# Larger field loads on the software queue, lent as output tiles until they are needed

## The chip, the core and the metric

The kernel runs on one core of a Trainium2 chip. A core has TensorE (PE) for matrix products, VectorE (DVE), ScalarE (ACT) and GpSimd (POOL) for elementwise work, and SyncE (SP), which here only issues DMA transfers. Transfers between the off-chip memory and the on-chip memory (128 partitions) are carried by sixteen DMA engines. A transfer can be issued from SyncE or ScalarE (the hardware queues q1 and q10 of the profile) or from GpSimd (the software queue q0). The metric is the device time of one execution in microseconds; lower is better. The kernel before takes 747.88 us (median of three runs, 745.85 to 748.31).

## The reference

There are 1024 samples with 32 fields of 128 numbers each, and for each of the 496 pairs of fields i < j a matrix W of 128x128:

```python
v_i = inputs[:, I_IDX, :]
v_j = inputs[:, J_IDX, :]
transformed = jnp.einsum('bpd,ped->bpe', v_i, W)
return transformed * v_j
```

For every pair the field i is multiplied by the pair's matrix and the result, element by element, by the field j. All is in float32. The inputs are 49 MB, the output is 260 MB.

## The kernel before, in words

**Tiles.** Everything is transposed: the 128 numbers of a field lie on the partitions and the 1024 samples along the row. A field is a tile of 128x1024 floats (512 KB), a weight load brings the matrices of eight pairs (`WL = 8`, 512 KB), and an output tile holds the results of four pairs (`OG = 4`, 2 MB). The pairs are taken with i from 30 down to 0 and j from i+1 to 31, numbered q = 0 to 495. So the fields with high numbers are needed first, and a field f is first needed when i reaches it: for fields 16, 12, 8 and 4 at the pairs 105, 171, 253 and 351. Each pair is done in two halves of 512 samples; half number u belongs to pair u // 2.

**A half.** For the first 15 pairs one matrix product in float32 is used (L203). After that, products are made of three parts: field and weights are each split into a high, a low and a difference part. `split_w` (L127 to L136) does this for two pairs' weights: ScalarE makes the high part (L132), GpSimd the others (L133 to L135). `split_x` (L141) does it for a field in two halves: ScalarE at L147, GpSimd at L148, L149 and, for later fields, L153; for the earlier ones VectorE makes the difference (L261). `first(u)` runs two of the products (L206) and ScalarE scales the sum in the accumulator (L207). `second(u - LAG)`, three halves later, adds the third product (L215), and VectorE multiplies by the field j into the output tile (L221). Two halves after a tile's last multiplication ScalarE issues its store (L254).

**Order.** The order is written by hand: the loop at L230 goes over the halves and appends to each engine's instructions (`tc.manual_schedule()`). Each engine works through its own in order and waits by semaphores where data or a buffer isn't ready. The splits are taken from a list, one per pair, by the pair at which they are allowed and the pair at which they are due. The splits of a field i may come at the earliest one pair after the row of i+1 has begun.

**Buffers.** Output tiles come from a pool of three (`opool`, L81), raw weight chunks from a pool of three (`rpool`), split weights from a pool of four. Each field has a tile of its own for the whole run.

**Loads.** Fields 30 to 15 and field 0 come one by one through SyncE or ScalarE (`load_x`, L86). Fields 1 to 14 come two at a time by `load_x_apart` (L109), and seven weight chunks (`WAPART`, L39) in the same way, by `load_apart` (L105): the first 112 rows are issued from GpSimd (L106), arranged so that the outermost dimension is `NE = 14`, and the other 16 rows from SyncE (L107). The host reorders those rows beforehand, so that the kernel reads them back in place. Three pairs later `move_on` (L101) issues a scrap of a load, with two rows, from GpSimd (L103). It has no use as data: [...] The first such call has five rows and the last has 13. All other weight chunks come whole from SyncE (L123), up to 12 pairs ahead of use.

Of the kernel before, what the change touches and what calls it, by code (L numbers as in the profile page):

```python
# [7 lines left out]
F32 = mybir.dt.float32  # L8
# [3 lines left out]
P = 128  # L12
NF = 32
NQ = NF * (NF - 1) // 2
BT = 1024
HB = 512
WC = 2
WL = 8
OG = 4
# [7 lines left out]
XAFTER = 54  # L27
XLEAD = 5

NE = 14
ROWS = 8 * NE
XAPART = 14
XSTEP, XPOS = 4, 8
WAPART = (45, 47, 49, 51, 54, 58, 60)  # L39
BACK = 3  # L40
SLAG = 2


# [6 lines left out]
def kernel(  # L50
# [26 lines left out]
    xpool = ctx.enter_context(tc.tile_pool(name="x", bufs=1))  # L77
    spool = ctx.enter_context(tc.tile_pool(name="xs", bufs=2))
    rpool = ctx.enter_context(tc.tile_pool(name="wr", bufs=WB))
    wpool = ctx.enter_context(tc.tile_pool(name="ws", bufs=4))  # L80
    opool = ctx.enter_context(tc.tile_pool(name="o", bufs=3))  # L81
    ppool = ctx.enter_context(tc.tile_pool(name="ps", bufs=8, space=bass.MemoryType.PSUM))

    x_sb = {}

    def load_x(f, pieces=1, eng=None):  # L86
        if f == 0:

            t = rpool.tile([P, WL, P], F32, tag="w", name="x_0").rearrange("p q e -> p (q e)")
        else:  # L90
            t = xpool.tile([P, BT], F32, tag=f"x{f}", name=f"x_{f}")
        s = BT // pieces
        for k in range(pieces):
            (eng or nc.sync).dma_start(out=t[:, k * s : (k + 1) * s], in_=xt[f, :, k * s : (k + 1) * s])
        x_sb[f] = t
# [5 lines left out]
    def move_on(k):  # L101

        nc.gpsimd.dma_start(out=mark[: 2 * k], in_=xt[0, : 2 * k, :16].rearrange("(b a) n -> a b n", a=k))  # L103

    def load_apart(dst, src):  # L105
        nc.gpsimd.dma_start(out=dst[:ROWS], in_=src[:ROWS].rearrange("(b a) m n -> a b m n", a=NE))  # L106
        nc.sync.dma_start(out=dst[ROWS:], in_=src[ROWS:])  # L107

    def load_x_apart(f):  # L109

        t = xpool.tile([P, 2, BT], F32, tag=f"x{f}", name=f"x_{f}")
        rows = xt[f : f + 2].rearrange("m d b -> (m d b)").rearrange("(d m b) -> d m b", m=2, b=BT)
        load_apart(t, rows)
        for k in range(2):
            x_sb[f + k] = t[:, k, :]

    def load_w(c, splits=(0, WL), eng=nc.sync):
        w_raw[c] = rpool.tile([P, WL, P], F32, tag="w", name=f"w_{c}")
        if c in WAPART:
            load_apart(w_raw[c], wt[c])  # L120
            return
        for a, b in zip(splits, splits[1:]):
            eng.dma_start(out=w_raw[c][:, a:b, :], in_=wt[c, :, a:b, :])  # L123
# [33 lines left out]
    first_q = {i: q for q, (i, j) in reversed(list(enumerate(pairs)))}  # L157
# [30 lines left out]
    w_q = {c: q for q, c in w_at.items()}  # L188
    back = []


    ctx.enter_context(tc.manual_schedule())
    po, ots, stores = {}, {}, []


    def first(u):
        q, h = divmod(u, 2)
        i, c = pairs[q][0], q // WC
        r = slice(q % WC * P, (q % WC + 1) * P)
        s = slice(h * HB, (h + 1) * HB)  # L200
        po[u] = ppool.tile([P, HB], F32, tag="po", name=f"po_{u}")
        if q < nq0:
            nc.tensor.matmul(po[u], w_raw[q // WL][:, q % WL, :], x_sb[i][:, s], start=True, stop=True)  # L203
        else:
            for t in (0, 1):
                nc.tensor.matmul(po[u], w_s[c][t][:, r], x_s[i][t][:, s], start=t == 0, stop=t == 1)  # L206
            nc.scalar.mul(po[u], po[u], 1.0 + EPS)  # L207

    def second(u):
        q, h = divmod(u, 2)  # L210
        i, j = pairs[q]
        r = slice(q % WC * P, (q % WC + 1) * P)
        s = slice(h * HB, (h + 1) * HB)
        if q >= nq0:
            nc.tensor.matmul(  # L215
                po[u], w_s[q // WC][2][:, r], x_s[i][2][:, s], start=False, stop=True, skip_group_check=True
            )
        g, k = divmod(q, OG)
        if k == 0 and h == 0:
            ots[g] = opool.tile([P, OG, BT], F32, tag="ot", name=f"ot_{g}")  # L220
        nc.vector.tensor_tensor(ots[g][:, k, s], po.pop(u), x_sb[j][:, s], ALU.mult)  # L221
        if q >= NQ - 2:
            stores.append((u + SLAG, out[g, :, k, s], ots[g][:, k, s]))
        elif g == 0 or q >= NQ - OG:
            if h == 1:
                stores.append((u + SLAG, out[g, :, k], ots[g][:, k]))
        elif k == OG - 1 and h == 1:
            stores.append((u + SLAG, out[g], ots[g]))

    for u in range(2 * NQ + LAG + SLAG):  # L230
        q = u // 2
        if u < 2 * NQ:
            i, j = pairs[q]
            if u % 2 == 0 and j == i + 1 and XAPART < i - 2 - XLEAD:
                load_x(i - 2 - XLEAD)
            first(u)
            if u == 2 * nq0:
                move_on(5)
            f = i - XSTEP
            if u % 2 == 0 and 0 < f < XAPART and f % 2 == 1 and j == i + XPOS:  # L240
                load_x_apart(f)
                back.append(q + BACK)
            if u % 2 == 1 and q in w_at:
                load_w(w_at[q])
                if w_at[q] in WAPART:
                    back.append(q + BACK)
            if u % 2 == 0 and q in back:
                move_on(16 - NE if q < w_q[WAPART[-1]] else 13)
            if u == 2 * x_at + 1:
                load_x(0)  # L250
        if LAG <= u < 2 * NQ + LAG:
            second(u - LAG)
        while stores and stores[0][0] <= u - LAG:
            nc.scalar.dma_start(*stores.pop(0)[1:])  # L254
        if u % 2 == 1:
            ready = [t for t in todo if t[0] <= q]
            if ready:
                ready[0][2](u)
                todo.remove(ready[0])
        while later and later[0][0] <= u:  # L260
            nc.vector.tensor_tensor(*later.pop(0)[1:], ALU.subtract)  # L261
# [35 lines left out]
```

## Time and profile before

| what | value |
|---|---|
| time, median of three | 747.88 us |
| span of the profiled execution | 749.5 us |
| bytes moved by DMA | 310.05 MB, 260.05 MB of them written to the off-chip memory |
| mean DMA rate | 414 GB/s |
| output stores of 2 MB | 122 of 132 stores |
| loads of 14 engines from GpSimd | 7 of two fields, 7 of weights |
| output multiplication (L221), one half | 684 ns, 992 of them |
| TensorE clock granted | full, but for the last slice |

How to read the page: its first part gives each engine's busy time and share; the second cuts the span in 40 slices, with a digit of tenths for each engine and for the mean of the sixteen DMA engines, and the rate in GB/s below. The third lists the DMA queues with packets, megabytes and the share of sixteen engines' time that their packets took. The list of waits has the waiting engine and line, the releaser after the arrow, and then the total in us, the number of times and the longest. The list of issues has the number of transfers, the KB of each, and the median time from issue to landing. A table of stretches has, for each engine, busy time and instruction count, then the granted clock, the DMA share and the rate.

### The profile page before, as it was taken

The page shows a single profiled execution, that of the slowest core. Times are in us where ns is not written, and L with a number is a line of the kernel's source. Part 1 is how long each engine was busy: PE and PEld are TensorE (multiplying, and loading weights), DVE is VectorE, ACT ScalarE, POOL GpSimd, SP SyncE. Part 2 cuts the span into 40 slices and gives each one's busy share as a digit, 9 for nine tenths or more (in the row PEclk, how much of TensorE's full clock was granted, in tenths as well). Part 3 has the DMA queues.
Part 4 walks back from the last instruction along what each step waited for, and adds up shares of the span by engine and source line. Part 5 has one row for each costly group of instructions (what it writes and reads, how often), then busy time and mean ns, then how long its engine had stood idle before and what let it go on. Part 6 is the DMA issues. An engine that isn't in the chain of part 4 may idle for free.

```text
span 749.5 us, 11006 instructions
## 1 busy us (share of the span) xinstructions
PE 701.5 (94%) x2946; PEld 549.5 (73%) x2946; DVE 643.9 (86%) x1012; ACT 626.7 (84%) x1256; POOL 611.1 (82%) x892
## 2 busy tenths in 40 slices
PE   7999999998999999999999999999999999999994
PEld 2477778776777778777777877777787777777783
DVE  3899999997988878879879888988898989788894
ACT  1198889997898889889888988888898898888893
POOL 1789999999998998988979797889788979697760
PEclk9999999999999999999999999999999999999998
DMA  9999999999999999999999999999999999999998
GB/s 347 426 426 420 432 415 409 419 414 418 412 387 430 414 424 421 423 424 425 427 408 427 428 405 430 425 420 406 420 405 421 401 428 398 429 420 415 401 410 339
DMA packets 32957, 310.05 MB, mean 414 GB/s; under 512 B 4480, under 2 KB 4608, under 8 KB 16384
## 3 DMA queue, kind: packets, MB, share of 16 engines
q10 hardware_dynamic: 19584, 261.10, 82.9%
q1 hardware_dynamic: 10816, 38.61, 13.3%
q0 software_dynamic: 2496, 9.64, 3.6%
q8 instruction: 24, 0.39, 0.2%
q14 instruction: 37, 0.30, 0.1%
HBM read 49.29 MB, written 260.05 MB: 413 GB/s over the span
## 4 chain that ended last, share of the span: by engine, by line
PE 50%; DMA 25%; POOL 14%; DVE 6%; issue 2%; ACT 1%; DVEq 0%; SPq 0%; POOLq 0%; ACTq 0%
PE po L206 32%; DMA out_dram<-ot 25%; PE po L215 15%; DVE ot L221 5%; PE po L203 4%; POOL wl L133 3%; POOL xd L153 3%; POOL xl L148 3%; POOL wd L135 2%; POOL xl L149 2%; POOL wd L134 1%; DMA x<-in_xt_dram 1%; ACT po L207 1%; ACT wh L132 1%; DVE xd L261 0%
## 5 line engine op out<-in xcount | busy, mean ns | idle before, releaser
L221 DVE TENSOR_TENSOR ot<-po,x 128x512 f32<-128x512 f32 x992 | 627.7, 684 | 96.1 <-DMA out_dram<-ot 56.9
L207 ACT ACTIVATE po<-po 128x512 f32<-128x512 f32 x962 | 545.2, 583 | 88.6 <-PE po L206 43.9
L206 PE MATMUL po<-xl,wl 128*128 128x512 f32 x962 | 377.8, 393 | 16.8 <-POOL wl L133 16.5
L206 PE MATMUL po<-xh,wh 128*128 128x512 f32 x962 | 378.1, 393 | 13.3 <-DVE ot L221 13.0
L215 PE MATMUL po<-xd,wd 128*128 128x512 f32 x962 | 375.0, 390 | 2.7 <-DVE xd L261 2.7
L206 PEld LDWEIGHTS po<-xh,wh 128*128 128x128 f32 x962 | 180.5, 188 | 63.3 <-DVE ot L221 25.1
L206 PEld LDWEIGHTS po<-xl,wl 128*128 128x128 f32 x962 | 180.6, 188 | 62.4 <-POOL wl L133 25.4
L133 POOL TENSOR_TENSOR wl<-w,wh 128x256 fp32r<-128x256 f32 x241 | 181.0, 751 | 54.9 <-ACT wh L132 49.7
L215 PEld LDWEIGHTS po<-xd,wd 128*128 128x128 f32 x962 | 180.6, 188 | 41.3 <-ACT po L207 2.1
L135 POOL TENSOR_TENSOR wd<-wl,wd 128x256 fp32r<-128x256 f32 x241 | 178.0, 739 | 20.1
L134 POOL TENSOR_SCALAR wd<-wh 128x256 fp32r<-128x256 f32 x241 | 99.3, 412 | 20.5
L132 ACT ACTIVATE wh<-w 128x256 fp32r<-128x256 f32 x241 | 99.3, 412 | 8.4 <-DVE ot L221 7.2
L148 POOL TENSOR_TENSOR xl<-x,xh 128x512 fp32r<-128x512 f32 x52 | 67.7, 1303 | 18.1 <-ACT xh L147 17.9
L153 POOL TENSOR_TENSOR xd<-xh,xl 128x512 fp32r<-128x512 f32 x32 | 41.3, 1292 | 2.7
L147 ACT ACTIVATE xh<-x 128x512 fp32r<-128x512 f32 x52 | 32.5, 629 | 11.6 <-DMA x<-in_xt_dram 11.5
L149 POOL TENSOR_SCALAR xl<-xl 128x512 fp32r<-128x512 f32 x52 | 34.6, 665 | 4.6
L203 PE MATMUL po<-x,w 128*128 128x512 f32 x60 | 30.6, 670 | 4.2 <-DMA x<-in_xt_dram 4.2
L203 PEld LDWEIGHTS po<-x,w 128*128 128x128 f32 x60 | 12.4, 212 | 21.7 <-issue 14.7
L261 DVE TENSOR_TENSOR xd<-xh,xl 128x512 fp32r<-128x512 f32 x20 | 19.2, 959 | 0.0
L103 POOL DMA_DIRECT2D mark<-in_xt_dram x15 | 9.6, 640 | 0.0
L106 POOL DMA_DIRECT2D w<-in_wt_dram x7 | 4.4, 624 | 0.0
L106 POOL DMA_DIRECT2D x<-in_xt_dram x7 | 4.4, 622 | 0.0
(5 smaller groups left out, 1.7 us busy)
## 6 DMA issues: line engine op xcount, KB each, us to landing
out_dram<-ot ACTq DMA_DIRECT2D x122, 2048.0 KB, 11.5
w<-in_wt_dram SPq DMA_DIRECT2D x54, 512.0 KB, 10.4
x<-in_xt_dram SPq DMA_DIRECT2D x16, 512.0 KB, 10.0
x<-in_xt_dram POOLq DMA_DIRECT2D x7, 896.0 KB, 14.0
w<-in_wt_dram POOLq DMA_DIRECT2D x7, 448.0 KB, 12.6
out_dram<-ot ACTq DMA_DIRECT2D x6, 512.0 KB, 8.8
x<-in_xt_dram ACTq DMA_DIRECT2D x4, 256.0 KB, 5.8
out_dram<-ot ACTq DMA_DIRECT2D x4, 256.0 KB, 7.0
```

The lines of the kernel that those rows point to most:

```text
L132: nc.scalar.mul(h, raw, 1.0 - 2.0**-13)
L133: nc.gpsimd.tensor_tensor(l, raw, h.bitcast(F32), ALU.subtract)
L134: nc.gpsimd.tensor_scalar(d, h.bitcast(F32), EPS, 1.0, ALU.mult, ALU.mult)
L135: nc.gpsimd.tensor_tensor(d, l.bitcast(F32), d.bitcast(F32), ALU.subtract)
L148: nc.gpsimd.tensor_tensor(l, x_sb[f][:, s], h.bitcast(F32), ALU.subtract)
L149: nc.gpsimd.tensor_scalar(l, l.bitcast(F32), 1.0 / EPS, 1.0, ALU.mult, ALU.mult)
L153: nc.gpsimd.tensor_tensor(d, h.bitcast(F32), l.bitcast(F32), ALU.subtract)
L203: nc.tensor.matmul(po[u], w_raw[q // WL][:, q % WL, :], x_sb[i][:, s], start=True, stop=True)
L206: nc.tensor.matmul(po[u], w_s[c][t][:, r], x_s[i][t][:, s], start=t == 0, stop=t == 1)
L207: nc.scalar.mul(po[u], po[u], 1.0 + EPS)
L215: nc.tensor.matmul(po[u], w_s[q // WC][2][:, r], x_s[i][2][:, s], start=False, stop=True, skip_group_check=True)
L221: nc.vector.tensor_tensor(ots[g][:, k, s], po.pop(u), x_sb[j][:, s], ALU.mult)
```

## The change

Fields 1 to 16 are now loaded in four groups of four (`load_group`, 1792 KB from GpSimd and 256 KB from SyncE each), so that a row of a group is 16 KB, like a row of an output tile. Fields 15 and 16 are now in a group, too. The groups are issued at the pairs 52 (fields 13 to 16), 141 (9 to 12), 219 (5 to 8) and 313 (1 to 4). Twelve weight chunks instead of seven are loaded on fourteen engines; the five new ones (12, 16, 24, 34, 38) lie in the first part of the run.

A group's tile has the size of an output tile. Until 20 pairs (`OWAIT`) before its load it serves as one: `out_tile` picks, of the three output tiles and the group tiles still free, the one that was used longest ago. So seven tiles serve for output up to pair 32, six up to 121, five up to 199, four up to 293, and three after that. On-chip memory stays the same. The aim is to let stores lie deeper in the queue during the first part, and to even out what the sixteen DMA engines carry.

```diff
-XAPART = 14
-XSTEP, XPOS = 4, 8
-WAPART = (45, 47, 49, 51, 54, 58, 60)
+XG = 4
+WAPART = (12, 16, 24, 34, 38, 45, 47, 49, 51, 54, 58, 60)
+XAT = (313, 219, 141, 52)
+OWAIT = 20
...
-    opool = ctx.enter_context(tc.tile_pool(name="o", bufs=3))
+    opool = ctx.enter_context(tc.tile_pool(name="o", bufs=1))
...
-    def load_x_apart(f):
-
-        t = xpool.tile([P, 2, BT], F32, tag=f"x{f}", name=f"x_{f}")
-        rows = xt[f : f + 2].rearrange("m d b -> (m d b)").rearrange("(d m b) -> d m b", m=2, b=BT)
-        load_apart(t, rows)
-        for k in range(2):
-            x_sb[f + k] = t[:, k, :]
+    def load_group(k):
+        t = xpool.tile([P, XG, BT], F32, tag=f"g{k}", name=f"x_g{k}")
+        f = XG * k + 1
+        load_apart(t, xt[f : f + XG].rearrange("m d b -> (m d b)").rearrange("(d m b) -> d m b", m=XG, b=BT))
+        for m in range(XG):
+            x_sb[f + m] = t[:, m, :]
...
+    until = {f"g{k}": q - OWAIT for q, k in group_at.items()}
+    used = {t: n - 9 for n, t in enumerate(("s0", "s1", "s2", *sorted(until, reverse=True)))}
+
+    def out_tile(g):
+        t = min((t for t in used if (g + 1) * OG <= until.get(t, NQ + OG)), key=used.get)
+        used[t] = g
+        pool = xpool if t in until else opool
+        return pool.tile([P, OG, BT], F32, tag=t, name=f"ot_{g}")
...
-            ots[g] = opool.tile([P, OG, BT], F32, tag="ot", name=f"ot_{g}")
+            ots[g] = out_tile(g)
...
-            if u % 2 == 0 and j == i + 1 and XAPART < i - 2 - XLEAD:
+            if u % 2 == 0 and j == i + 1 and XG * ngroup < i - 2 - XLEAD:
                 load_x(i - 2 - XLEAD)
...
-            f = i - XSTEP
-            if u % 2 == 0 and 0 < f < XAPART and f % 2 == 1 and j == i + XPOS:
-                load_x_apart(f)
+            if u % 2 == 0 and q in group_at:
+                load_group(group_at[q])
                 back.append(q + BACK)
```

On the host the rows of fields 1 to 16 are reordered in fours instead of twos.

More of the change, by code (lines that the diff above doesn't have):

```diff
@@ L189 @@
     back = []
+    ngroup = NF // XG // 2
+    group_at = {q: k for k, q in enumerate(XAT)}
+    assert all(q < first_q[XG * k + XG + 1] for q, k in group_at.items())
+    until = {f"g{k}": q - OWAIT for q, k in group_at.items()}
[5 more added lines that the diff above has]
+        return pool.tile([P, OG, BT], F32, tag=t, name=f"ot_{g}")
     ctx.enter_context(tc.manual_schedule())
@@ L274 @@
     xt = _np.ascontiguousarray(x.transpose(1, 2, 0))
-    for f in range(1, XAPART, 2):
-        two = xt[f : f + 2].transpose(1, 0, 2).copy()
-        two[:ROWS] = two[:ROWS].reshape(NE, 8, 2, BT).transpose(1, 0, 2, 3).reshape(ROWS, 2, BT).copy()
-        xt[f : f + 2] = two.reshape(2, P, BT)
+    for f in range(1, XG * 4, XG):
+        some = xt[f : f + XG].transpose(1, 0, 2).copy()
+        some[:ROWS] = some[:ROWS].reshape(NE, 8, XG, BT).transpose(1, 0, 2, 3).reshape(ROWS, XG, BT).copy()
+        xt[f : f + XG] = some.reshape(XG, P, BT)
     wt = _np.ascontiguousarray(w[perm].reshape(NQ // WL, WL, P, P).transpose(0, 3, 1, 2))
```

## The prediction

> **What bounds the kernel now.** I read the page first: engines, slices, queues, the chain, the costliest groups. Five resources are within reach of the end, so the engine rows alone decide nothing:
>
> ```profile
> PE 701.5 (94%) x2946; PEld 549.5 (73%) x2946; DVE 643.9 (86%) x1012; ACT 626.7 (84%) x1256; POOL 611.1 (82%) x892
> ...
> DMA  9999999999999999999999999999999999999998
> GB/s 347 426 426 420 432 415 409 419 414 418 412 387 430 414 424 421 423 424 425 427 408 427 428 405 430 425 420 406 420 405 421 401 428 398 429 420 415 401 410 339
> DMA packets 32957, 310.05 MB, mean 414 GB/s; under 512 B 4480, under 2 KB 4608, under 8 KB 16384
> ...
> q10 hardware_dynamic: 19584, 261.10, 82.9%
> q1 hardware_dynamic: 10816, 38.61, 13.3%
> q0 software_dynamic: 2496, 9.64, 3.6%
> ```
>
> The reader is to see that the DMA row is full from the first slice to the last but one, and that the shares of the queues (stores q10, SyncE loads q1, software loads q0) add up to 99.8% of sixteen engines' time, with 0.3% more for instruction fetches. Nothing else is as full as this. Then the waits and the issues:
>
> ```profile
> DVE ot L221 <- DMA out_dram<-ot: 56.9, 48, 3.0
> ...
> out_dram<-ot ACTq DMA_DIRECT2D x122, 2048.0 KB, 11.5
> x<-in_xt_dram POOLq DMA_DIRECT2D x7, 896.0 KB, 14.0
> w<-in_wt_dram POOLq DMA_DIRECT2D x7, 448.0 KB, 12.6
> ```
>
> VectorE waits 48 times for a store to give an output tile back; a store lands 11.5 us after its issue, about two stores' worth of transfer (2.1 MB at 414 GB/s is 5.07 us). Two stores lie in the queue while VectorE fills the third tile. So compute runs ahead until the tiles are full and then follows the DMA. Last, stretches of 25 us:
>
> ```profile
> 200.00:225.00 25.00, 23.19 (x102) 18.53 (x101) 20.44 (x32) 21.81 (x45) 23.25 (x34) 1.00 1.01 397
> 225.00:250.00 25.00, 24.00 (x105) 19.17 (x104) 21.36 (x36) 22.22 (x45) 22.38 (x33) 1.00 1.01 429
> 275.00:300.00 25.00, 25.00 (x112) 20.52 (x111) 21.46 (x36) 23.20 (x47) 20.72 (x33) 1.00 1.01 422
> 500.00:525.00 25.00, 22.73 (x99) 18.20 (x98) 20.36 (x33) 20.92 (x42) 22.95 (x37) 1.00 1.00 405
> ```
>
> The DMA share stands at 1.00 to 1.01, but the rate differs, 397 to 429: some packets take longer in stretches that hold a software load (at 220 us and at 522 us in the first and the last of these lines, none in the two between). PE did 112 matmuls in one stretch against some 103 as a rule, so compute can go about 9% faster than it is allowed to.
>
> From the trace's packet records I worked out three more numbers. A store packet of 16 KB takes 611 ns at the median and 621 on average; an 8 KB packet of a software load 309 and 343; a 4 KB one 159 and 195, and of a SyncE load 159 and 168. Time above the median pace adds up to 19 us of the run, mean over engines. Between 30 and 735 us the engines were without a packet for only 1.4 us each. And the sixteen completions of one store spread by about 2 us early on, while from 550 us on one engine ends 3 to 4.7 us behind the middle one.
>
> [...] 16 KB in 611 ns on 16 engines is 429, and the best slice shows 432. [...] a weight load's eight 4 KB packets per engine, alternating with eight store packets, are 8 x (159+611) = 6.2 us of its 12.6 to landing; a field load's are 8 x (309+611) = 7.4 of 14.0. Both leave 6.4 to 6.6 us. [...] after the field load at 323 us two engines stand 2.3 us ahead of the middle, and by 352 us most of it is gone. The two that are spared are slower than the rest, or carry more.
>
> **The change, part by part.**
>
> *Stores and bytes.* Nothing is added or taken away: 310 MB either way. With the DMA full, only what changes packet time, idle time or the ending counts.
>
> *Fields.* Seven 896 KB software loads, their seven 128 KB rests and two 512 KB SyncE loads (fields 15, 16) become four of 1792 KB and four rests. The rows become 16 KB. At median pace 896 packets of 309 and 256 of 159 ns (317.6 us) become 512 of 611 (312.8): 4.8/16 = 0.3 us less.
>
> *Weights.* Five more loads go from SyncE to the software queue.
>
> *Cost of a software load.* Two readings. The 14 loads' own time above pace is 3.4 us, and stores beside them lose 5.2, together 0.6 each. The stretches with one average about 414 GB/s, those without 422: 8/422 of 25 us is 0.5 each. I take 0.5; field loads cost no more than weight loads half their size (412 against 415 GB/s), so I count loads, not bytes. Sixteen instead of 14: +1.0 us. The other bound, by bytes (12.85 MB for 9.64): 8.6 x 0.33 = +2.9. The SyncE loads that go (seven whole ones) lost about 0.1 us each themselves and 0.1 in stores beside them: 7 x 0.2 = -1.4.
>
> *Relief of two engines.* One 14-way load gives each of 14 engines eight packets. Before: 56 x 343 + 56 x 195 ns = 30.1 us that the spared two don't do. After: 32 packets of 16 KB at about 630 and 96 x 195 = 38.9. So 8.8 us more, and from pair 52 on instead of 98. The laggard's 3 to 4.7 us should go. What that is worth is bounded: the idle 1.4 us of the middle, and in the ending about 1.0 (the last store's latest engine is 1.6 us behind the middle one, the next 1.0 and 0.6). Lower bound 0, since much of the idle may be compute's own. I take both: -2.4. Too much relief costs little: 8.8 us on two of sixteen, if all idle, is +1.1.
>
> *Output tiles.* Seven to pair 32, six to 121, five to 199, four to 293, then three. This takes away part of VectorE's 56.9 us of waiting, some 25 to 30 us of it before 440 us. But its wait is for the full DMA, so I cost it at nothing: the stores ahead in the queue hide it. What it does buy is depth when a four-field load takes half of every engine for 8 x (611+611) = 9.8 us.
>
> *New waits.* The group load on GpSimd, and its rest on SyncE, now wait for the last stores from their tile. Behind GpSimd's stand the weight splits (L133 to L135), for which PE waits. The tile's last group ends 20 pairs earlier; store issue comes about 2.5 pairs after that and GpSimd is at most 3 pairs ahead: 14.5 pairs at 1.5 us (749.5/496) are 22 us. With five tiles at most four stores are queued, 4 x 5.9 = 24 us; with four, 18. So 0 to 2 us at one or two loads, under a queue that holds over 12 us of work: nothing.
>
> *Lead of the loads.* Three of the groups are issued 13 pairs, 20 us, before the first split that reads them may run (pairs 154, 232, 326). I expect landing after 9.8 + 6.5 = 16 us. Before, the lead was 23 to 47 pairs. Three microseconds late would be hidden by the queue; 15 would not.
>
> Sum: -0.3 + 1.0 - 1.4 - 2.4 = -3.1, so **744.8 us**.
>
> **Rivals.**
> 1. *No gain, 747.2.* The idle engines of the middle were compute's doing and the laggard costs nothing, as stores wait in the queue behind it: -0.3 + 1.0 - 1.4 = -0.7, with the noise of the three runs (745.85 to 748.31). For it: the full share in every stretch leaves little to win. Against it: the 3 to 4.7 us of one engine late in the run.
> 2. *Slower, 751.5.* Time above pace goes with bytes (+2.9), the spared engines now idle (+1.1), and a late group stalls ScalarE at the split (L147), and with it PE, until the queue drains in part; with -1.4 for the SyncE loads a loss of 3.6 needs only 1 us from three stalls. For it: the lead shrinks from 23 to 47 pairs to 13, and the 397 stretch shows a bad load. Against it: 4 us of slack and a queue of two or three stores.
> 3. *Larger gain, 740.* Lost time goes by packets: 448 instead of 784 long ones for the fields, and the laggard was what slowed the stores too. Half of the 8.6 us around software loads goes, beside the 3.1: 740.5. For it: 14% of the 8 KB packets were late by some 245 ns each. Against: five more weight loads with just the packets that 9% of were late.
>
> **How the numbers follow.** Forecast 43%, no gain 26%, slower 17%, larger gain 14%. The forecast lies 0.4% below the 747.88 of before with about 2 us to each side, so a quarter of it falls within 0.3% (above 745.6); of the no-gain case about 70% does, the rest splits. Faster 0.32 + 0.14 + 0.05 = 0.51; same 0.11 + 0.18 = 0.29, and slower 0.20 with what is left of both. The range must reach to most of the 740 case and past the no-gain one, and leaves out the worse half of the slower one: 740.0 to 751.0.
>
> **What would show it.** Right: the page lists four field loads of 1792 KB and 12 weight loads from GpSimd; VectorE's waits on stores shrink before 440 us and stay after; the DMA share stays at 1.00 or more; late in the run no engine's completion trails by over 2 us; mean rate about 416 GB/s. Field loads land in 15 to 18 us. Wrong if ScalarE's split (L147's line) waits for field data after the start, if GpSimd waits long for stores at a group load, if the DMA share falls below 1.00 in a middle stretch, or if the stretches with group loads fall well below 400 GB/s.

## The result, and the profile after

The changed kernel takes 757.65 us (median of four runs, 757.02 to 758.18), the kernel before on the same chips 747.35 (745.85 to 748.31): a ratio of 1.0130, 95% interval 1.0111 to 1.0149. It is slower by some 10 us. The forecast was 744.8, the range ended at 751.0.

The page of the changed kernel, with the lines that answer to those shown of before:

```profile
PE 702.2 (93%) x2946; PEld 556.7 (74%) x2946; DVE 670.5 (89%) x1012; ACT 626.2 (83%) x1256; POOL 613.1 (81%) x896
...
DMA  9999999999999999999999999999999999999998
GB/s 344 427 428 426 389 383 430 426 425 415 422 378 377 421 431 417 425 419 391 429 426 418 422 382 431 369 370 417 419 388 420 418 421 429 409 430 422 426 429 354
...
q10 hardware_dynamic: 19584, 261.10, 82.3%
q1 hardware_dynamic: 9872, 35.39, 12.5%
q0 software_dynamic: 2848, 12.86, 4.9%
```

The DMA is as full as before, with the same bytes. What has changed is the rate: outside the dips most slices stand at 415 to 431 GB/s, as good as before, but there are pairs of slices at 389 and 383, 378 and 377, 369 and 370. The issues say what lies there:

```profile
x_g<-in_xt_dram POOLq DMA_DIRECT2D x4, 1792.0 KB, 18.2
w<-in_wt_dram POOLq DMA_DIRECT2D x12, 448.0 KB, 11.3
```

The groups' loads are issued at 95, 228, 343 and 480 us from the software queue, and their last 16 rows, from SyncE, at 79, 210, 327 and 474. Three of the four pairs of loads fall on these pairs of slices (of 18.9 us each): the first slice holds SyncE's rows, the second one the others, which in the last pair begin in the first slice already. The loads at 327 and 343 us fall on slices at 419 and 391. Stretches around the loads (columns as before):

```profile
75.00:100.00 25.00, 24.05 (x106) 19.30 (x105) 25.00 (x40) 23.08 (x48) 23.09 (x33) 1.00 1.01 399
100.00:125.00 25.00, 22.46 (x98) 17.65 (x96) 23.25 (x36) 21.06 (x44) 23.07 (x32) 1.00 1.01 395
225.00:250.00 25.00, 22.25 (x90) 17.37 (x89) 20.14 (x30) 18.55 (x38) 20.56 (x30) 0.93 1.01 390
475.00:500.00 25.00, 17.36 (x77) 14.06 (x75) 14.64 (x23) 16.70 (x34) 17.37 (x29) 0.93 1.01 349
```

The share is 1.01 and the rate 349 to 399: the engines are busy all the time, but their packets take longer. In the last stretch PE does 77 matmuls instead of some 103, for VectorE waits for a store:

```profile
DVE ot L227 <- DMA out_dram<-ot: 20.5, 13, 9.7
...
ACT xh L142 <- DMA x_g<-in_xt_dram: 5.2, 2, 3.3
```

VectorE's wait for stores fell from 56.9 us to 20.5, as the lent tiles were to bring about, but one of the waits is now 9.7 us long. Group data came late twice, for 5.2 us in all.

From the packet records I took two sums, in us and as means over the sixteen engines: time above the median pace of a packet of its size, and time without a packet from the first one to the last (most of that lies at the start). Together they account for the spans (with the same bytes that is bookkeeping: it says where the time went, not why):

| kernel | above pace | without a packet | sum against before | span against before |
|---|---|---|---|---|
| before | 19.0 | 16.8 | | (749.5) |
| changed | 25.7 | 17.0 | +6.9 | +6.6 |
| changed, groups whole from SyncE | 14.6 | 17.2 | -4.0 | -4.2 |
| changed, no tiles lent | 32.8 | 19.8 | +16.8 | +16.6 |

So the change lost its time in slow packets, not in idle engines. The profiled execution of before is one of its longer ones (spans of the timed ones are 743 to 751 us), so the traces show 6.6 us where the runs give 10.

The slow packets are those of the group loads. A 16 KB packet of a store takes 611 ns at the median; those of the groups took 770 on average from the software queue (448 packets) and 1059 from SyncE (64, the last 16 rows of each group). (448 x 159 + 64 x 448)/16 engines is 6.2 us. What runs beside them is slowed as well: between the first and the last packet of a group load, stores took 703 ns on average and SyncE's 4 KB packets 228, for 613 and 161 beside the groups of the third row of the table. By this count the seven loads of two fields of the kernel before lost 6.0 us (1.8 their own, 4.2 beside them), and the four group loads 13.2 (6.2 and 6.9). The 7.1 us more are as much as the whole rise of the time above pace (6.7).

### The profile page after: what moved, and what is told of

Same layout as the page of the kernel before. It is cut to its first block, busy times and chain, and to the rows that moved or that the text cites. A ratio compares the mean times of both kernels' runs of the same rounds, so it can differ in the third digit from the quotient of the medians.

```text
span 756.1 us, 11007 instructions
## 1 busy us (share of the span) xinstructions
PE 702.2 (93%) x2946; PEld 556.7 (74%) x2946; DVE 670.5 (89%) x1012; ACT 626.2 (83%) x1256; POOL 613.1 (81%) x896
## 4 chain that ended last, share of the span: by engine, by line
PE 70%; POOL 13%; DMA 9%; DVE 4%; issue 2%; ACT 0%; DVEq 0%; POOLq 0%; ACTq 0%
PE po L212 44%; PE po L221 22%; DMA out_dram<-ot 6%; PE po L209 4%; DVE ot L227 4%; POOL wl L128 3%; POOL xd L148 3%; POOL xl L143 2%; DMA x_g<-in_xt_dram 2%; POOL wd L130 2%; POOL xl L144 1%; POOL wd L129 1%; DMA x<-in_xt_dram 1%; DVE xd L266 0%; ACT po L213 0%
## 5 line engine op out<-in xcount | busy, mean ns | idle before, releaser
L227 DVE TENSOR_TENSOR ot<-po,x 128x512 f32<-128x512 f32 x720 | 477.8, 689 | 51.2 <-PE po L221 22.4
L212 PEld LDWEIGHTS po<-xh,wh 128*128 128x128 f32 x962 | 182.4, 190 | 48.7 <-DVE ot L227 10.2
L227 DVE TENSOR_TENSOR ot<-po,x_g 128x512 f32<-128x512 f32 x272 | 176.8, 688 | 24.5 <-PE po L221 13.3
L129 POOL TENSOR_SCALAR wd<-wh 128x256 fp32r<-128x256 f32 x241 | 99.2, 412 | 20.5
L143 POOL TENSOR_TENSOR xl<-x_g,xh 128x512 fp32r<-128x512 f32 x32 | 41.5, 1296 | 4.4 <-ACT xh L142 4.4
L143 POOL TENSOR_TENSOR xl<-x,xh 128x512 fp32r<-128x512 f32 x20 | 25.8, 1292 | 15.6 <-ACT xh L142 15.3
L142 ACT ACTIVATE xh<-x_g 128x512 fp32r<-128x512 f32 x32 | 20.2, 632 | 5.2 <-DMA x_g<-in_xt_dram 5.2
L142 ACT ACTIVATE xh<-x 128x512 fp32r<-128x512 f32 x20 | 12.4, 628 | 11.3 <-DMA x<-in_xt_dram 11.1
## 6 DMA issues: line engine op xcount, KB each, us to landing
x_g<-in_xt_dram POOLq DMA_DIRECT2D x4, 1792.0 KB, 18.2
```

What stands on the lines that cost most here:

```text
L129: nc.gpsimd.tensor_scalar(d, h.bitcast(F32), EPS, 1.0, ALU.mult, ALU.mult)
L143: nc.gpsimd.tensor_tensor(l, x_sb[f][:, s], h.bitcast(F32), ALU.subtract)
```

## The experiments

Theory A says that the groups' long packets are what costs; rivals were the short lead and the burst (B), five more software loads (C), and the lending (D). Why the packets are slow was a question of its own: the order of rows in off-chip memory (E), the software queue (F), or the blocks in which the rows are given (G, formed after runs 9 and 10). Ratios are to the kernel before on the same chip, with their 95% intervals.

**1. Two loads of 8 KB rows, at the same place.** Between the two stands a mark of two rows.

```diff
-        load_apart(t, xt[f : f + XG]...)
+        for m in (2, 0):
+            load_apart(t[:, m : m + 2, :], xt[f + m : f + m + 2]...)
```

> The changed kernel, but each group of four fields comes in two loads of two fields (rows of 8 KB), issued one right after the other at the same pair into the same tile. Theory A (reading rows of 16 KB is slow: 770 ns a packet on the software queue and 1059 on SyncE's, for 611 of a store's; (448 x 159 + 64 x 447)/16 = 6.2 us): packets of 8 KB go back to about 340 ns, the time falls by 6 us or more, to 748 to 751 us. Theory B (so much field data at one place, with a short lead, starves compute): nothing changes, 756 to 758 us. Theory C (five more weight loads on the software queue): nothing changes either.

751.21 us, 1.0033 (1.0021 to 1.0045). The software packets took 340 ns on average (309 at the median). 6.4 us came back from the row length alone, at the same place, with the same bytes (but for the marks) and the same lead. A holds; B and C alone could not have given this. That A's 6.2 us has the same size is in part luck: the groups' own packets still lost 3.0 us here, 3.2 less, and the packets beside them 3.6, which is 3.3 less.

**2. Rows 16 KB long, 20 KB apart in memory.** The groups come from an array of their own, padded.

> The changed kernel, with the rows of the groups still 16 KB long, but 20 KB apart in memory instead of 16 KB. If theory A's slow reads come from the distance between rows that the engines read side by side, packets go back to about 620 ns and the time to 748 to 751 us; if they come from the length of a row, packets stay near 770 ns and the time at 757. Theories B and C: 757.

756.28 us, 1.0103 (1.0077 to 1.0129), packets 770 ns and 1104. The distance between rows isn't it, as far as this one step from 16 to 20 KB shows.

**3. Seven weight chunks on fourteen engines.**

```diff
-WAPART = (12, 16, 24, 34, 38, 45, 47, 49, 51, 54, 58, 60)
+WAPART = (45, 47, 49, 51, 54, 58, 60)
```

> The changed kernel with the old seven weight chunks on fourteen engines instead of twelve. Theory C (the five new weight loads cost 0.5 us or more each): 754 to 755 us. Theory A: 757 or a little above, since the two spared engines are less relieved. Theory B: 757.

756.16 us, 1.0094 (1.0065 to 1.0123). In the direction of C, by 1 to 3 us, but the interval overlaps with the changed kernel's: inconclusive by itself. Run 7 tries C in the kernel before.

**4. No tiles lent.**

```diff
-        t = min((t for t in used if (g + 1) * OG <= until.get(t, NQ + OG)), key=used.get)
+        t = min((t for t in ("s0", "s1", "s2") if ...), key=used.get)
```

> The changed kernel with three output tiles all along; the group tiles aren't lent. Theory D (lending itself harms, by new waits of the loads on stores, or by stores that pile up): the time falls by 3 us or more. Theory A: 757 to 759 us, since three tiles hide the slow loads worse than four to seven. Theory B: slower than 757, since three tiles leave compute waiting sooner.

768.42 us, 1.0259 (1.0234 to 1.0284). D is refuted the other way round: lending saves about 10 us in the changed kernel. Its stretches and waits show what lies behind:

```profile
100.00:125.00 25.00, 20.18 (x79) 15.10 (x78) 16.70 (x29) 17.31 (x36) 20.47 (x29) 0.93 1.00 383
...
350.00:375.00 25.00, 20.13 (x79) 16.08 (x78) 16.41 (x27) 16.89 (x34) 17.22 (x27) 0.86 0.99 394
...
500.00:525.00 25.00, 18.25 (x72) 14.35 (x70) 15.26 (x25) 15.51 (x33) 13.26 (x18) 0.86 0.98 390
```

```profile
DVE ot L227 <- DMA out_dram<-ot: 51.7, 34, 8.4
```

With three tiles VectorE stands still at three of the four groups (PE does 72 to 79 matmuls in 25 us), and the DMA share falls below 1. That is the smaller part, though: by the table of sums above, idle engines make 2.8 us of the difference to the changed kernel and slower packets 7.1, and by the count of packets beside the groups these lie elsewhere (13.4 us there, for 13.2). Why packets away from the groups are slower with three tiles isn't shown.

**5. and 8. The two 8 KB loads ten pairs apart; and the groups eight pairs earlier as well.** The edits are `load_group(k, m)` called at q and q + 10, and `XAT = (305, 211, 133, 52)`.

> As the two 8 KB loads, with the second load of each group (its two lower fields) ten pairs after the first instead of right behind it. It is still open why two 8 KB loads end at 751.2 us and not at the 748.2 of before. If 1.8 MB at one place is what is left (half of every engine for some 10 us), the time falls to about 748 us; if the five weight loads or the lending are, it stays at 751.

> As the spread loads, with groups 0 to 2 issued eight pairs earlier (305, 211, 133), so that their first fields have 21 pairs instead of 13 before they are split. If late data still costs (ScalarE waited 5.2 us for group data in the changed kernel), 1 to 3 us faster than with the spread loads alone; if the lead is long enough with rows of 8 KB, the same.

752.34 us, 1.0051 (1.0031 to 1.0071), and 751.87, 1.0039 (1.0024 to 1.0055): no better than run 1. Neither the burst nor the lead is what remains once rows are 8 KB long.

**6. Groups whole from SyncE, rows of 16 KB in plain order.**

```diff
-        load_apart(t, xt[f : f + XG]...)
+        nc.sync.dma_start(out=t, in_=xt[f : f + XG]...)
```

> The changed kernel with each group loaded whole by SyncE, 128 rows of 16 KB on all sixteen engines; the software queue has only the weights. If long rows are slow to read whoever issues them, the packets of the groups take 750 ns or more and the time stays at 755 us or above; if the software queue is what makes them slow, they take 611 to 630 ns and the time goes to 750 us or below (bar what the missing relief of two engines costs, 20 us of work on two of sixteen, at most 2.5 us).

747.43 us, 0.9993 (0.9978 to 1.0008): as fast as before. The packets took 636 ns. The four loads are in flight from 78 to 98 us, 208 to 224, 321 to 341 and 468 to 487. The stretches around them:

```profile
75.00:100.00 25.00, 23.99 (x105) 19.26 (x104) 25.00 (x39) 23.01 (x48) 23.07 (x32) 1.00 1.01 429
200.00:225.00 25.00, 23.82 (x105) 19.40 (x105) 23.55 (x36) 22.48 (x46) 22.73 (x33) 1.00 1.01 405
320.00:345.00 25.00, 23.82 (x106) 19.40 (x105) 22.86 (x35) 22.38 (x46) 22.49 (x33) 1.00 1.00 427
465.00:490.00 25.00, 20.88 (x91) 16.66 (x90) 18.59 (x30) 19.18 (x38) 19.97 (x32) 1.00 0.98 401
```

Two of the four stretches stand at 429 and 427 GB/s. In the second one the load's packets took 707 ns on average; in the last one they took 613, and the share of 0.98 tells of idle engines. In three of the four loads, then, the mean is 612 to 614 ns, where the changed kernel's four on the software queue have 699 to 840: rows of 16 KB in one load of 2 MB aren't slow as such. Nor is the landing quicker (19.4 us). It is how the transfer is given that matters.

**7. The kernel before, with twelve weight chunks.**

> The kernel before, with the twelve weight chunks of the change on fourteen engines instead of seven. If a software load costs 0.5 us more than SyncE's, 750.5 us; if the relief of the two slow engines pays, 746 to 747; if neither, 748.

751.82 us, 1.0047 (1.0028 to 1.0066): 3.5 us for five loads (2 to 5 by the interval), 0.7 each. C holds beside A, in the kernel before. It would fit what separates runs 1, 5 and 8 from the kernel before (1.0033 to 1.0051), but none of them was run with seven chunks.

**9. and 10. The order of rows and the queue, crossed.** Run 9 leaves the groups on the software queue and puts each block's eight rows together in memory; run 10 gives SyncE's load in sixteen blocks, with the rows of one block sixteen rows apart in memory.

```diff
+        nc.gpsimd.dma_start(out=t[:ROWS], in_=xg[k, :, : 8 * XG * BT].rearrange("a (b m n) -> a b m n", b=8, m=XG))
```

```diff
+        nc.sync.dma_start(out=t, in_=rows.rearrange("(b a) m n -> a b m n", a=16))
```

> The changed kernel with the groups still on the software queue and fourteen engines in rows of 16 KB, but each engine's eight rows lie together in memory (blocks of 132 KB) instead of fourteen engines reading fourteen neighbouring rows. Theory E (what is slow is that neighbouring long rows are read at once by different engines): the software queue's 16 KB packets take about 630 ns instead of 770, and the time falls by 4 us or more, to 750 to 753. Theory F (the software queue reads long rows slowly): packets and time stay at 770 ns and 756 us.

> The other corner: groups whole from SyncE on sixteen engines, as in the run before that took 747.4 us, but with sixteen engines reading sixteen neighbouring rows of 16 KB. Theory E: SyncE's 16 KB packets go from 636 to 750 ns or more (the rests of the changed kernel took 1059 in this order), and the time rises to 753 us or above. Theory F: packets stay near 636 ns and the time at 747.

Run 9: 757.25 us, 1.0126 (1.0098 to 1.0154), packets 762 ns. Run 10: 751.83 us, 1.0050 (1.0031 to 1.0069), packets 776 ns. Run 9 speaks against E, run 10 against F. So a third thing sets the two slow orders apart from run 6. In runs 9 and 10, as in the change, the transfer is given in blocks of eight rows; in run 6 the rows are one plain dimension of 128. Theory G: the blocks are what slows the packets. That fourteen blocks went to fourteen engines shows in the completions: of the sixteen of a group's software load in the changed kernel, two came 6.6 to 11.7 us before the middle one, the others within 1.8 us of it. Why blocks should slow the packets isn't shown; the traces have no number of an engine. Nor are the blocks all of it: the rests, 16 plain rows each, took from 775 (run 18) to 1283 ns (run 4) on average, and 1059 in the changed kernel.

**13., 14. and 15. Blocks with rows in order; and smaller blocks on the software queue.** Run 13 is run 6 in sixteen blocks of eight, each block's rows together. Runs 14 and 15 keep the software queue and the interleaved rows, with loads of 32 (28) rows in eight (seven) blocks of four; run 15 has seven weight chunks.

```diff
+        nc.sync.dma_start(out=t, in_=xg[k, :, : 8 * XG * BT].rearrange("a (b m n) -> a b m n", b=8, m=XG))
```

```diff
+        for p in (0, 64, 32, 96):
+            nc.gpsimd.dma_start(out=t[p : p + 32], in_=rows[p : p + 32].rearrange("(b a) m n -> a b m n", a=8))
```

> Groups whole from SyncE on sixteen engines, each engine's eight rows together in memory (as in the run with 636 ns a packet) but given as sixteen blocks of eight partitions (as in the run with 776). Theory E (neighbouring rows in off-chip memory read at once): 636 ns and 747 us. Theory G (blocks of eight partitions: [...]): 760 ns or more and 751 to 752 us.

> The changed kernel with each group on the software queue as four loads of 32 rows, eight engines with four partitions each, [...]. Neighbouring rows are still read at once by neighbouring engines, rows are 16 KB, and the queue is the software one; twelve weight chunks as in the change. Theory G: packets of about 630 ns and 748 to 752 us (no relief of two engines by the groups). Theory E or F (software queue): 760 ns and 756 us or above.

> As an attempt at a better version: groups on the software queue in four loads of 28 rows on seven engines with four partitions each, [...] the other 16 rows in four small loads from SyncE, and the old seven weight chunks. Theory G: 16 KB packets of about 630 ns on the software queue, and 745 to 749 us, since relief and number of weight loads are as before. If packets stay at 760 ns, G is wrong: 755 or above.

| groups' 16 KB packets | queue | a block's rows in memory | given in | median, mean ns | time us |
|---|---|---|---|---|---|
| changed | software | apart | blocks of 8 | 760, 770 | 757.65 |
| run 9 | software | together | blocks of 8 | 738, 762 | 757.25 |
| run 10 | SyncE | apart | blocks of 8 | 726, 776 | 751.83 |
| run 13 | SyncE | together | blocks of 8 | 668, 735 | 751.15 |
| run 6 | SyncE | in order | plain rows | 611, 636 | 747.43 |
| run 14 | software | apart | blocks of 4 | 611, 692 | 763.34 |
| run 15 | software | apart | blocks of 4 | 611, 678 | 767.13 |

Run 13 has ratio 1.0043 (1.0028 to 1.0058): but for rows that lie in an array of their own, all is as in run 6, and blocks make the packets 99 ns slower and the run by about 4 us. G's 760 ns was too much, its time was right. Runs 14 and 15 take the blocks of eight away on the software queue, and the median goes back to 611, though the means stay above the 630 that was expected. They also have only seven or eight blocks to a load, and that fewer long packets at once are what helped them isn't ruled out. The median follows the blocks, in all seven rows (668 to 760 ns in blocks of eight, 611 without them), and neither queue nor order.

The time doesn't follow it alone. Against run 6, blocks of eight cost 4 us from SyncE (runs 10 and 13) but 10 from the software queue (the changed kernel and run 9). Most of that stands in the packets again: beside the groups, SyncE's 4 KB packets took 228 and 205 ns in these two, and 163 in runs 10 and 13. Why the blocks cost more from the software queue wasn't tried.

The times of runs 14 (1.0205, 1.0164 to 1.0247) and 15 (1.0250, 1.0216 to 1.0284) were a miss. A wait of run 14 tells why:

```profile
ACT xh L146 <- DMA x_g<-in_xt_dram: 15.9, 2, 8.8
```

The last of its four loads landed up to 23.2 us after issue, with 13 pairs (20 us) of lead. Here B was right, for a version that I had made.

**16., 17. and 18. A longer lead** for runs 14 and 15, and for the changed kernel itself.

```diff
-XAT = (313, 219, 141, 52)
+XAT = (297, 203, 125, 52)
```

> As the four loads of 32 rows on eight engines each, with groups 0 to 2 issued 16 pairs earlier (297, 203, 125). There the packets were at 611 ns at the median, as theory G has it, but the last loads landed up to 23 us after issue and ScalarE waited 15.9 us for group data, twice. If that lateness made the time (763), it falls to 748 to 752 us with the same packets; if it stays above 756, the four loads cost something else.

> As the four loads of 28 rows on seven engines each with seven weight chunks, with groups 0 to 2 issued 16 pairs earlier. If lateness made its 767 us, 746 to 752.

> The changed kernel itself with groups 0 to 2 issued 16 pairs earlier, with its blocks and 16 KB rows as they are. Theory G: the packets stay near 770 ns and the time at 754 to 757 us, for in the changed kernel ScalarE waits only 5.2 us for group data. Theory B (a lead of 13 pairs starves compute): 750 us or below.

Run 16: 754.14 us, 1.0073 (1.0044 to 1.0102), 9 us less than run 14, with the packets as there (611 at the median). Run 17: 756.17, 1.0101 (1.0076 to 1.0126), 11 us less than run 15. Lateness was most of it, but both miss what was expected by 2 to 4 us; they have 28 and 23 transfers on the software queue besides the marks, and what those cost wasn't tried by itself. Run 18: 758.28 us, 1.0126 (1.0096 to 1.0157), packets 771 ns on the software queue: a longer lead doesn't help the changed kernel. For it, B is refuted.

**11. and 12. Run 6 with seven weight chunks; run 6 without lending.**

> Groups whole from SyncE and the tiles lent, with the old seven weight chunks on fourteen engines. Five more weight loads on the software queue cost the kernel before 3.5 us (1.0047). If they cost the same here, 744 us, faster than before; if they pay by the relief of two engines, 748 or more.

> Groups whole from SyncE with the twelve weight chunks, three output tiles all along. In the changed kernel the lending was worth 10.8 us (768.4 without). If it is worth this because a large load takes half of every engine for 10 us or more, whatever its packets, the loss is as large here, 755 us or above; if it only hid the slow reads, 748 to 750.

Run 11: 751.88 us, 1.0055 (1.0033 to 1.0077), a miss in sign. Its page:

```profile
DMA  9999999999999999999999997999999999999997
GB/s 348 422 424 427 421 427 425 429 425 419 425 394 425 429 426 430 427 425 413 408 421 401 429 397 305 399 426 432 416 412 428 418 425 403 426 426 424 414 409 311
```

The 305 with a 7 above it is an idle DMA; the pages of run 6 and of the changed kernel have no such slice. By the completions of stores between 340 and 445 us, one engine ends 7 to 10 us behind the middle one and a second 3 to 5; in run 6 one ends 4 to 6 us behind. The mean time without a packet is 23.2 us instead of run 6's 17.2. By my estimate, from the 195 ns that a packet of a weight load took in the kernel before (56 of them, or 96), seven weight loads keep about 11 us of work off two engines and twelve about 19; for groups whole from SyncE I count none. So relief would be worth 4 to 5 us here, where it is missing. The estimate takes every load to spare the same two engines, which the traces don't show. That it is relief which makes these 4 to 5 us is argued from the completions; in run 7, with the field loads' relief beside it, five more loads only cost.

Run 12: 752.13 us, 1.0050 (1.0018 to 1.0083): lending is worth some 4 us with plain 2 MB loads, and some 10 with loads in blocks. That is between what the two theories gave.

## Why the prediction was wrong

*The bound* was read rightly: the DMA stays full, and the span grows by what its packets take longer.

*Fields, "at median pace ... 512 of 611": this step failed.* I priced the group's packets at the pace of a store's 16 KB packet, and said that "field loads cost no more than weight loads half their size, so I count loads, not bytes". They took 770 and 1059 ns: +6.2 us where the sum has -0.3. The allowance of 0.5 us for what a software load loses, itself and beside it, failed with it: counted with its rest, with stores and SyncE's loads beside it, a group lost 3.3 us, and a load of two fields 0.9 before. Run 1 gave 6.4 us back from the row length alone. The row of an 8 KB packet (309 at the median, 343 on average) was on the table, yet could not show it: 8 KB packets in blocks keep that median in the runs as well (means of 340 to 361); why they do isn't shown. I took a store, which reads on-chip memory, for the nearest row of a load that writes to it. Run 6 shows that the pace was possible (611 at the median, 636 on average), but only for a load given as 128 plain rows.

*Cost of a software load, "+1.0 us" less "1.4" for SyncE's loads.* The weights' part was mis-sized too: five loads moved cost 3.5 us in the kernel before (run 7), 0.7 each on top of what SyncE's cost, against 0.3 each in my sum (0.5 less 0.2). In the changed kernel taking them back gave 1 to 3 us, not clear of noise (run 3), and beside run 6 taking them back cost 4 to 5 (run 11). So up to 2 us of the error may lie here.

*Relief, -2.4.* None of it came. That each load spares the same two engines was my assumption. The laggard did go (from 600 us on no engine ends more than 2.2 us behind the middle one), but after the group load at 228 us the two spared engines stood 8 us ahead of the rest, and time without a packet stayed as it was, 17.0 for 16.8. At the end the last store's latest engine is 1.4 us behind the middle one, for 1.6 before.

*Output tiles, at nothing.* As a step of the sum this was wrong in the other direction: without the lending the changed kernel takes 768.4. I had named what it buys (depth under a four-field load) and then given it no number.

*New waits and lead.* Right for the change: GpSimd doesn't appear in the waits for stores, and 16 pairs more lead brought nothing (run 18). The landing was 18.2 us where 16 was expected, and it was late twice, for 5.2 us. That, and stretches with group loads at 349 to 399 GB/s, are two of the signs of being wrong that I had named.

*The rivals.* The slower one had the direction, and 751.5 for its time; its causes (stalls at the split, idle spared engines) weren't those. Its bound by bytes, 2.9 us for the loads, was too low as well: that its time is nearer is luck.

Together: the groups and what runs beside them make 7.1 us more than the field loads before. The rest of the 10.3 us could be the weights' 3.5, but run 7 measured these in the kernel before, and the sum of the two is argued.

## What to carry to other kernels

Where the DMA is the bound, price a transfer by packets that go the same way, between the same memories and given in the same form, and count what it does to the packets beside it: here a store's 611 ns was the load's pace as 128 plain rows (612 to 614 in three loads of run 6), and not in blocks of eight (735 to 776). If a transfer is cut into blocks to choose its engines, keep rows short: among the groups in blocks of eight on the software queue, those with 8 KB rows lost least (751.21 us in run 1, 757.65 with 16 KB rows). Look at the spread of one store's completions before moving work off slow engines: five more loads on fourteen engines cost 3.5 us in run 7.

## What the runs showed of the hardware

Long rows weren't slow to load: 2 MB as 128 plain rows of 16 KB went at 636 ns a packet beside stores (429 and 427 GB/s in two of the four stretches of run 6), and at 612 to 614 in three loads of four. The same rows in blocks of eight partitions took 735 to 776, and slowed the stores beside them from 613 to between 658 and 703. That the blocks are the cause rests on the pattern of seven runs; how they slow the packets isn't shown.

A software load's packets shared the engines with those of stores: in the kernel before, beside the 112 packets of one load, 90 to 168 packets of stores went for the six two-field loads that stood alone (7.6 to 11.2 us from the first packet to the last), and 97 to 159 for the last six of weights (6.1 to 10.0 us). The prediction's 7.4 and 6.2 us, with one store packet for each, are near the shortest of them.

The changed kernel's TensorE clock fell to half five times before its end, four times for 3.4 us and once for 6.8 (0.93 in two of the stretches of 25 us shown), and not once before the end in the kernel before; the mean was 0.982 against 0.996. It cost nothing that these runs show: run 6 has 0.987 and is as fast as before.

Open remain: why a software load of 448 KB cost 0.7 us more than the same from SyncE in the kernel before, why blocks of eight slow 16 KB packets, and cost some 6 us more from the software queue than from SyncE, what holds runs 16 and 17 at 754 and 756 us, and why the mean of the software packets in blocks of four (673 to 692 ns) stays above SyncE's 636 with the median equal.

No version beat the kernel before: groups whole from SyncE, with lent tiles and twelve weight loads, equals it (0.9993, 0.9978 to 1.0008).
